# First image of a fused attention kernel: the next input loaded at unit 16, and the split weights made in units without row turns or statistics, those of v partly on GpSimd

## The chip, the cores and the metric

The kernel runs on one core of a Trainium2 chip. The metric is the device time of one execution in microseconds (us), the median over repeated runs. Times inside the kernel are read from one profiled execution; they are counted from the start of its span.

The engines that matter here are TensorE (PE in the profile; its weight loads are PEld), VectorE (DVE), ScalarE (ACT), GpSimd (POOL) and SyncE (SP), whose queue issues nearly all DMAs of this part, strictly in order: an issue that waits for a semaphore holds up all issues behind it.

## The reference, cut to what matters

Two layers over 8 images of 384 channels and 32 x 32 pixels. The change lies in layer 0, an attention with 8 heads of 48 over the 1024 pixels, with a bias that depends on the relative position alone:

```
x   = x + L0(_gn(x), ...)            # _gn: group norm over 32 groups

qkv  = tokens @ qkv_w + qkv_b                       # q, k, v
attn = einsum('bhnd,bhmd->bhnm', q * scale, k)
attn = softmax(attn + relative_bias(h, w, ...), axis=-1)
out  = einsum('bhnm,bhmd->bhnd', attn, v)
out  = out @ proj_w + proj_b
```

Layer 1 (a second attention and a feed-forward block with weights reduced to signs) follows and is not touched.

## The kernel before, in words

Layer 0 is `_layer0`. Images are worked on one after the other. The attention of an image is cut into 32 units, numbered 0 to 31: 4 pairs of heads, two halves of the queries, four groups of keys. Unit u has these steps:

- `scores`: 16 matmuls on TensorE (L746) into two PSUM tiles `s`, one for each head of the pair;
- two additions on VectorE (L757), each of 128 x 1024 elements, that put `s` plus a window of the bias table `grow` into two SBUF tiles `e`;
- two exponentials on ScalarE (L761), in place in `e`;
- `weigh`: 16 matmuls (L777) of `e` with v. TensorE does the weighing of unit u-2 behind the scores of unit u (LAG = 2).

PSUM holds four tiles of this size. One collects the output `o`, so three are left for scores, and the second score tile of a unit takes the place of the first one of the unit before. TensorE can therefore start the scores of unit u+1 only when the first addition of unit u is done.

Everything else is put between the units by an order written out by hand. `later.after(n, work)` issues `work` at the n-th following `later.step()`, and there is one step at the end of every unit. The instructions of such work then stand on each engine's queue behind those of the unit. In the first image (b = 0) this work is:

- **Row pieces and row turns.** The bias table is built while it is in use. `grow_load` (L486) fetches a piece of the table from DRAM with 4 DMAs of 117 KB, in the first image's units into a part of `oT`, and `grow_turn` (L496 on ScalarE, L498 on VectorE, one piece in two each) copies it, with its columns turned round, into `grow`. The last 16 pieces are loaded at the end of v's projection and of the units 0 to 14, and turned two or three units later, on VectorE behind the units 0, 3, 5, 7, 9, 10, 12, 14 and 16.
- **Parts of the weights.** Later images multiply in a faster number format with weights and inputs split into a high part (L108, a mask), a low part (L134, a subtraction), a mix of both (L112), and the low part scaled (L142). For q and k `_cut_weights` does this in four stages for each third k of the rows (128 x 768), with a store of 393 KB to DRAM behind three of them (L122). For v `cut_weights_v` does it on 128 x 384, with stores of 197 KB. All of it is on VectorE.
- **The next input.** `load` (L343) fetches image 1 (three DMAs of 512 KB) into `xn`. `group_norm` then measures it (`bn_stats`, L513, on VectorE, two instructions for each of three stages), sends the statistics through DRAM (L517, L521), aggregates them (L527), computes on GpSimd, sends the result out and back (L535, L539), and applies it on ScalarE (L551).
- **Divisions.** At the end of each pair of heads `divide` sends the row sums through DRAM (L803, L805), inverts them on GpSimd (L806), spreads them by DMA (L810, L818) and multiplies on GpSimd (L822).

The tiles `e`, the mixed parts `cd` and the tiles `cv` of v's parts come from one pool of nine buffers (`etile`). An addition into a new `e` waits until the last user of its buffer is done, a DMA out of it included.

Each DMA on SyncE's queue signals one of eight semaphores in turn, and a DMA waits for the landing of the one eight places before it.

After the units of the first image, TensorE multiplies image 1 with the split weights: `cuts.load` (L161) is issued at unit 28, `wvh` (L986) after the last unit, into the buffer of `wv` itself, and `load_weights_v` (L687) behind that.

Of the kernel before, what the change touches and what calls it, by code (L numbers as in the profile page):

```python
# [22 lines left out]
ALU = mybir.AluOpType  # L23
# [6 lines left out]
B, C, IH, IW = 8, 384, 32, 32  # L30
N = IH * IW
KC = C // P
MT = N // P
HALF = 512
# [29 lines left out]
CUT = 4096.0  # L64
# [41 lines left out]
def _masked(nc, out, of):  # L106

    nc.vector.tensor_single_scalar(out.bitcast(INT), of.bitcast(INT), MASK, op=ALU.bitwise_and)  # L108


def _mixed(nc, out, low, high):
    nc.vector.scalar_tensor_tensor(out, low, -CUT, high, ALU.mult, ALU.add)  # L112


def _cut_weights(nc, k, w, tile, there):

    parts = {}

    def store(i):
        nc.sync.dma_start(  # L122
            there[:, :, i, k].rearrange("n p c -> p n c"),
            parts[i].rearrange("p (n c) -> p n c", c=P),
        )

    def high():
        parts[0] = tile("ch")
        _masked(nc, parts[0], w)
        store(0)  # L130

    def low():
        parts[1] = tile("cl")
        nc.vector.tensor_sub(parts[1], w, parts[0])  # L134

    def mixed():
        parts[2] = tile("cd")
        _mixed(nc, parts[2], parts[1], parts[0])
        store(2)

    def scaled():
        nc.vector.tensor_scalar_mul(parts[1], parts[1], CUT)  # L142
        store(1)

    return [high, low, mixed, scaled]
# [129 lines left out]
def _layer0(tc, ins, x1, sums, shared, weights, beside):  # L275
# [4 lines left out]
    nc = tc.nc  # L280
# [4 lines left out]
    with ExitStack() as ctx:  # L285
# [8 lines left out]
        def etile(name, shape=(P, N), dtype=F32):  # L294
            return ep.tile(list(shape), dtype, tag="e", name=name)
# [4 lines left out]
        later = _Later()  # L300
# [25 lines left out]
        for g in range(P // QT):  # L326
            at = g * QN
# [12 lines left out]
        def load(b):  # L340
            t = shared.image(f"xn{b}")
            for k in range(KC):
                nc.sync.dma_start(t[:, k], x[b, ts(k, P)].rearrange("p h w -> p (h w)"))  # L343
            return t

        first = load(0)
# [13 lines left out]
        wv = const.tile([P, KC, C], F32, tag="wv", name="wv")  # L360
# [236 lines left out]
        cut_v = dram.tile([P, 3, KC, C], F32, tag="cutv", name="cutv", bufs=1)  # L597

        def cut_tile(name):
            return etile(name)[:, 0 : 2 * C]  # L600

        def cut_weights_v(k):

            w = wv[:, k]
            t = etile(f"cv{k}")
            high, mixed = t[:, 0:C], t[:, HALF : HALF + C]

            def first():
                _masked(nc, high, w)
                nc.sync.dma_start(cut_v[:, 0, k], high)  # L610
                nc.vector.tensor_sub(w, w, high)

            def second():
                _mixed(nc, mixed, w, high)
                nc.sync.dma_start(cut_v[:, 2, k], mixed)
                nc.vector.tensor_scalar_mul(w, w, CUT)
                nc.sync.dma_start(cut_v[:, 1, k], w)

            first()
            later.after(2, second)  # L620

        class Ahead:

# [234 lines left out]
        def project_out(b, res, pairs):  # L858
            for m in range(KC):
                products(b, m, pairs)  # L860
                nc.vector.scalar_tensor_tensor(
                    res[m], flat2(pps[b, m]), bp[:, m : m + 1], res[m], ALU.add, ALU.add
                )
                nc.sync.dma_start(x1[b][ts(m, P), :], res[m])
# [4 lines left out]
        stages = group_norm(0, first)  # L869
# [37 lines left out]
        for i in range(len(parts) // 2):  # L907
            later.after(i + (13 if i < 9 else 12), lambda: grow_turns(1))
            at = 1 + i % NF0 if i < 12 else 2 + i % 2
# [4 lines left out]
        for k in range(KC):  # L914
            stages = _cut_weights(
                nc, k, plain[:, ts(k, 2 * C)],
                lambda name, k=k: (
                    spare if name == "ch" else plain[:, ts(k, 2 * C)] if name == "cl"
                    else cut_tile(f"{name}0{k}")
                ),  # L920
                cut,
            )
            for at, stage in zip(((9, 11, 13, 15), (20, 21, 22, 23), (24, 25, 26, 27))[k], stages):
                later.after(at + 1, stage)
        for k in range(KC):
            later.after(17 + k, lambda k=k: cut_weights_v(k))
        for b in range(B):
            held = []
            for i, u in enumerate(units):
                done = held.pop(0) if len(held) == LAG else None  # L930
                held.append(
                    (u, scores(b, qk, u, lambda: weigh(b, *done) if done else None))
                )
                if i == (12 if b == 0 else 1) and b + 1 < B:
                    xn = load(b + 1)
                    for at, stage in zip(
                        (5, 6, 7, 10, 13, *((14, 15) if b == 0 else (13, 13))),
                        group_norm(b + 1, xn),
                    ):
                        later.after(at, stage)  # L940
                if i == 3 and b > 0:
                    project_out(b - 1, residuals(b - 1, etile), range(NF0))
                if b == B - 1:
                    for at, work in beside:
                        if at == i:
                            work()
                later.step()
                if i == 28 and b == 0:
                    cuts = _Cut(
                        nc, cut, BLOCKS,  # L950
                        shared.pool.tile([P, KC * 3 * C], F32R, tag="w", name="wc"),
                    )
                    for n in range(BB):
                        cuts.load(n)
                if b in (1, 2, 3) and i == 12:
                    t = cut_tile(f"cw{b}")
                    weights.load_part(b - 1, t)
                    for at, stage in enumerate(
                        weights.cut(
                            b - 1, t, lambda name, b=b, t=t: t if name == "cl" else cut_tile(f"{name}1{b}")  # L960
                        )
                    ):
                        later.after(4 + at, stage)
                masks, rounds = ((28, 29, 31), ()) if b == 0 else ((25, 26, 27), (28, 29, 30))
                if b + 1 < B:
                    if i == masks[0]:
                        ahead = Ahead(b + 1, xn)
                    if i in masks:
                        ahead.mask(masks.index(i))
                    if i in rounds:  # L970
                        ahead.round(rounds.index(i))

            def weigh_held():
                finish = weigh(b, *held.pop(0))
                if finish is not None:
                    finish()

            if b + 1 == B:
                while held:
                    weigh_held()  # L980
                break
            order = [n % len(BLOCKS) for n in range(b % 2 * BB, b % 2 * BB + len(BLOCKS))]

            if b == 0:
                wh = const.tile([P, KC, C], F32R, tag="wv", name="wvh")
                nc.sync.dma_start(wh.bitcast(F32), cut_v[:, 0])  # L986
                for k in range(KC):
                    ahead.round(k)
            for k in range(2):
                ahead.low(k)  # L990
            weigh_held()
            ahead.low(2)
            ahead.load_weights_v(wh)
            weigh_held()
            for k in range(KC):
                ahead.mixed(k)

            def load_behind(n):
                if n in order[:BB]:
                    cuts.load((n + BB) % len(BLOCKS))  # L1000

            for n in order[:2]:
                for i in range(2):
                    ahead.products(cuts, n, i)
            for n in order[:2]:
                ahead.products(cuts, n, 2)
                ahead.take(n)
                load_behind(n)
            for at, n in enumerate(order[2:], 2):
                for i in (2, 0, 1):  # L1010
                    ahead.products(cuts, n, i)
                ahead.take(n)
                load_behind(n)
                if at == BB - 1:
                    for m2 in range(MT // 2):
                        ahead.project_v(m2)
            qk = ahead.qk
# [8 lines left out]
    def finish():  # L1026
        project_out(B - 1, rest, range(NF0, NP0))
        keep.close()
# [1341 lines left out]
```

## Time and profile before

| What | Value |
|---|---|
| Median of 3 runs | 2956.97 us (2955.67 to 2958.47) |
| The profiled execution: its own time, its span | 2955.07 us, 2953.0 us |
| TensorE busy | 2920.5 us, 99% of the span |
| VectorE busy | 1970.4 us, 67% |
| ScalarE busy | 1505.0 us, 51% |
| GpSimd busy | 491.5 us, 17% |
| Units of the first image: first and last score matmul's stretch | from 76 us to about 200 us |

Busy shares are averages over the whole kernel. The change touches only the 32 units of the first image, some 125 us of 2953, so views with a window on this stretch are the ones to read. In them one pair of L757 additions on VectorE marks one unit, and the distance from pair to pair is the time of a unit. A duration in the profile can reach some hundredths of a microsecond into the next instruction's, so times are best taken from start to start.

### The profile page before, as it was taken

To read this page: it belongs to the slowest core of one execution; us is meant where nothing else is said; L and a number is where in the kernel's file an instruction comes from. 1 tells how busy PE (TensorE), PEld (TensorE's weight loads), DVE (VectorE), ACT (ScalarE), POOL (GpSimd) and SP (SyncE) were. 2 spreads that over 40 slices of the span, in tenths; PEclk is the share of its full clock that TensorE was granted. 3 is DMA by queue.
4 is the path that set the end of the run, shared out by engine and by line. 5 is a ranking of instruction groups with operands and counts; after the bars stand their busy time and mean duration, and the time that the engine had idled before them with its cause. 6 is when DMAs were issued, how large, how long until landed. Compare 5 with 4: busy or idle time off the path is not lost.

```text
span 2953.0 us, 47525 instructions
## 1 busy us (share of the span) xinstructions
PE 2920.5 (99%) x19538; PEld 1694.0 (57%) x19538; DVE 1970.4 (67%) x2005; ACT 1505.0 (51%) x1846; POOL 491.5 (17%) x312
## 2 busy tenths in 40 slices
PE   8999999999999999999999999999999999999998
PEld 3345565657565666644545647647647647655553
DVE  3786858676676757664665775775875875875756
ACT  2553626354453626353553554555555555564644
POOL 2020202111110202112202202302302302301020
PEclk9999999999999999999999999999999999999999
DMA  7643141322213040323311212112112112112111
GB/s 197 175 132 99 45 128 39 114 59 69 76 47 98 24 128 17 93 82 97 87 56 31 83 32 72 67 31 72 67 32 71 67 32 72 67 40 83 40 46 39
DMA packets 131972, 214.36 MB, mean 73 GB/s; under 512 B 62145, under 2 KB 81073, under 8 KB 130369
## 3 DMA queue, kind: packets, MB, share of 16 engines
q1 hardware_dynamic: 128480, 209.39, 24.1%
q8 instruction: 157, 2.57, 0.4%
q10 hardware_dynamic: 3264, 1.82, 0.2%
q14 instruction: 71, 0.57, 0.1%
HBM read 161.83 MB, written 40.28 MB: 68 GB/s over the span
## 4 chain that ended last, share of the span: by engine, by line
PE 91%; DVE 3%; DMA 2%; ACT 2%; issue 1%; SPq 0%; POOL 0%; DVEq 0%; ACTq 0%
PE s L746 15%; PE o L777 15%; PE s L1722 11%; PE o L1771 11%; PE pg L170 6%; PE y2p L2016 6%; PE y1p L1965 5%; PE pp L845 4%; PE pv L1659 4%; PE pm L170 3%; PE pp L1868 3%; PE vg L698 2%; PE pq L1511 2%; PE pq L572 1%; PE vm L698 1%; DVE qk L1592 1%
## 5 line engine op out<-in xcount | busy, mean ns | idle before, releaser
L761 ACT ACTIVATE e<-e 128x1024 f32<-128x1024 f32 x512 | 534.6, 1057 | 347.9 <-DVE e L757 331.2
L757 DVE TENSOR_TENSOR e<-s,grow 128x1024 f32<-128x1024 f32 x512 | 601.3, 1218 | 162.4 <-PE s L746 144.8
L746 PE MATMUL s<-qk 48*64 48x512 f32 x4096 | 613.8, 592 | 7.2 <-DVE e L757 7.2
L777 PE MATMUL o<-e,v 64*64 64x512 f32 x4096 | 608.5, 590 | 1.6 <-DVE e L757 1.6
L1733 ACT ACTIVATE e<-s,kc 128x512 f32<-128x512 f32 x768 | 463.4, 693 | 172.9 <-PE s L1722 161.9
L1722 PE MATMUL s<-qk,qk 64*64 64x512 f32 x3072 | 418.8, 592 | 1.4 <-DVE oT L1781 1.2
L1771 PE MATMUL o<-e,v 64*64 64x512 f32 x3072 | 414.3, 590 | 0.0
L746 PEld LDWEIGHTS s<-qk 48*64 48x64 f32 x4096 | 229.5, 132 | 248.1 <-issue 102.2
L777 PEld LDWEIGHTS o<-e,v 64*64 64x64 f32 x4096 | 250.2, 133 | 196.4 <-issue 105.2
L1722 PEld LDWEIGHTS s<-qk,qk 64*64 64x64 f32 x3072 | 154.2, 132 | 191.0 <-issue 108.5
L1748 DVE TENSOR_TENSOR t<-t,e 128x1024 f32<-128x1024 f32 x192 | 230.9, 1221 | 45.7 <-ACT e L1733 45.5
L1771 PEld LDWEIGHTS o<-e,v 64*64 64x64 f32 x3072 | 160.0, 133 | 168.7 <-issue 141.6
L806 POOL TENSOR_TENSOR inv<-sums,over 128x16 f32<-128x16 f32 x32 | 96.2, 3008 | 850.3 <-DMA sums<-sd 783.3
L1952 DVE TENSOR_REDUCE parts<-y 128x1 f32<-128x1024 f32 x75 | 89.7, 1217 | 102.6 <-ACT y L1949 102.1
L1745 DVE TENSOR_TENSOR t<-e,e 128x1024 f32<-128x1024 f32 x96 | 114.1, 1224 | 57.7 <-ACT e L1733 57.7
L1628 POOL TENSOR_TENSOR hc<-hc,rsqrt 128x32 f32<-128x32 f32 x24 | 138.3, 5761 | 2.0
L1659 PE MATMUL pv<-wv,bx 128*128 128x384 f32 x384 | 128.3, 491 | 0.0
L1868 PE MATMUL pp<-oT,L_attn_proj_wT 128*128 128x512 f32 x288 | 126.3, 595 | 1.7 <-DVE oT L1834 1.7
L845 PE MATMUL pp<-oT,wp 128*128 128x512 f32 x288 | 125.7, 595 | 0.0
L1659 PEld LDWEIGHTS pv<-wv,bx 128*128 128x128 f32 x384 | 119.4, 314 | 9.8 <-ACT e L1733 4.1
L673 DVE SCALAR_TENSOR_TENSOR qk<-pg,qk 128x1024 f32<-128x1024 f32 x42 | 51.5, 1225 | 100.0 <-PE pg L170 73.9
L1965 PE MATMUL y1p<-lun,w 128*128 128x512 f32 x360 | 113.5, 396 | 2.4 <-DVE lun L1915 2.4
(225 smaller groups left out, 3581.5 us busy)
## 6 DMA issues: line engine op xcount, KB each, us to landing
rb<-rd SPq DMA_DIRECT2D x110, 256.0 KB
wc<-there SPq DMA_DIRECT2D x25, 576.0 KB
wc<-cut SPq DMA_DIRECT2D x24, 576.0 KB
xn<-in_x_dram SPq DMA_DIRECT2D x24, 512.0 KB
res<-in_x_dram SPq DMA_DIRECT2D x24, 512.0 KB
x<-res SPq DMA_DIRECT2D x24, 512.0 KB
bx<-x SPq DMA_DIRECT2D x8, 1536.0 KB
rq<-hi SPq DMA_DIRECT2D x48, 256.0 KB
```

The lines of the kernel that those rows point to most:

```text
L170: self.nc.tensor.matmul(out[:, h], w[:, i, k], part[k][:, ts(h, HALF)], start=(k == 0 and i != 1), stop=(k == KC - 1 and i != 0),)
L746: nc.tensor.matmul(s[j][ts(c, QP), i], qk[pair][rows, 1, ts(4 * m2 + 2 * i + c, QP)], qk[pair][rows, 0, ts(h, HALF)], start=True, stop=True,)
L757: nc.vector.tensor_add(e.rearrange("p (i q) -> p i q", i=2), s[j], bass.AP(near.tensor, near.offset, [near.ap[0], [-QROWS * IW, 2], [1, HA ...
L761: nc.scalar.activation(e, e, AF.Exp)
L777: nc.tensor.matmul(po[ts(j, S0), r], v[keys, 2 * m2 + i, 2 * pair + j, :], es[j][keys, ts(i, HALF)], start=(m2 == 0 and i == 0), stop=(m2 ...
L845: nc.tensor.matmul(pps[b, m][:, h], (wp[:, k] if k < NF0 else wl)[:, ts(m, P)], oT[:, k, ts(h, HALF)], start=(k == 0), stop=(k == (NF0 if ...
L1659: nc.tensor.matmul(pv[:, i, 0:C], xt[:, k].rearrange("c (p m) -> c m p", m=MT)[:, 2 * m2 + i], wv[:, k], start=(k == 0), stop=(k == KC - 1),)
L1722: nc.tensor.matmul(s[j][ts(c, QP), i], qk[pair, 1][rows, ts(4 * m2 + 2 * i + c, QP)], qk[pair, 0][rows, ts(h, HALF)], start=True, stop=True,)
L1733: nc.scalar.activation(e[:, ts(i, HALF)], s[j][:, i], AF.Exp, scale=kc[:, pair, j, m : m + 1])
L1748: nc.vector.tensor_add(total[j], total[j], e)
L1771: nc.tensor.matmul(po[ts(j, D1), r], v[keys, 2 * m2 + i, at : at + D1], es[j][keys, ts(i, HALF)], start=(m2 == 0 and i == 0), stop=(m2 == ...
L1965: nc.tensor.matmul(py[m][:, h], w1[:, k, ts(m, P)], un[k][i][:, ts(h, HALF)], start=(k == 0 and i == 0), stop=(k == KC - 1 and i == 1),)
```

## The change

Four things move, all of them in the first image, and some instructions change their engine:

- The load of image 1 is issued at unit 16 and not at unit 12. Its first two measurements come behind the units 17 and 18 (before: 16 and 17), the third with the gathering behind 19 (before: 18), and the aggregation stays behind 21. So does the application, behind 24, 25 and 26.
- The q and k parts: k = 0 at the units 10, 11, 15, 16 (before: 9, 11, 13, 15), k = 1 at 2, 4, 6, 8 (before: 20 to 23), k = 2 at 23, 24, 26, 27 (before: 24 to 27).
- The v parts, which were made in two steps behind the units 16 to 20, are now made in three steps: behind the units 17, 22, 23 for k = 0, behind 21, 25, 26 for k = 1, and behind 27, 30, 31 for k = 2. All stores move to the second and third step.
- Of the v parts, the subtraction and the scaling are on GpSimd; the mask and the mix stay on VectorE.

```diff
         def cut_weights_v(k):
-            w = wv[:, k]
-            t = etile(f"cv{k}")
-            high, mixed = t[:, 0:C], t[:, HALF : HALF + C]
+            w, tiles = wv[:, k], []
 
             def first():
+                tiles.append(etile(f"cv{k}"))
+                high = tiles[0][:, 0:C]
                 _masked(nc, high, w)
+                nc.gpsimd.tensor_sub(w, w, high)
+
+            def second():
+                high, mixed = tiles[0][:, 0:C], tiles[0][:, HALF : HALF + C]
                 nc.sync.dma_start(cut_v[:, 0, k], high)
-                nc.vector.tensor_sub(w, w, high)
-
-            def second():
                 _mixed(nc, mixed, w, high)
+                nc.gpsimd.tensor_scalar(w, w, CUT, 1.0, ALU.mult, ALU.mult)
                 nc.sync.dma_start(cut_v[:, 2, k], mixed)
-                nc.vector.tensor_scalar_mul(w, w, CUT)
+
+            def third():
                 nc.sync.dma_start(cut_v[:, 1, k], w)
 
-            first()
-            later.after(2, second)
+            return first, second, third
...
-            for at, stage in zip(((9, 11, 13, 15), (20, 21, 22, 23), (24, 25, 26, 27))[k], stages):
+            for at, stage in zip(((10, 11, 15, 16), (2, 4, 6, 8), (23, 24, 26, 27))[k], stages):
                 later.after(at + 1, stage)
-        for k in range(KC):
-            later.after(17 + k, lambda k=k: cut_weights_v(k))
+        for k, at in enumerate(((17, 22, 23), (21, 25, 26), (27, 30, 31))):
+            for when, stage in zip(at, cut_weights_v(k)):
+                later.after(when + 1, stage)
...
-                if i == (12 if b == 0 else 1) and b + 1 < B:
+                if i == (16 if b == 0 else 1) and b + 1 < B:
                     xn = load(b + 1)
                     for at, stage in zip(
-                        (5, 6, 7, 10, 13, *((14, 15) if b == 0 else (13, 13))),
+                        (2, 3, 4, 6, 9, 10, 11) if b == 0 else (5, 6, 7, 10, 13, 13, 13),
                         group_norm(b + 1, xn),
                     ):
                         later.after(at, stage)
```

## The prediction

> **What bounds the kernel now.** The page first: TensorE is busy all but 32 us of the span, so a gain must come out of waits of TensorE, or out of slow matmuls.
>
> ```profile
> span 2953.0 us, 47525 instructions
> PE 2920.5 (99%) x19538; PEld 1694.0 (57%) x19538; DVE 1970.4 (67%) x2005; ACT 1505.0 (51%) x1846; POOL 491.5 (17%) x312
> ```
>
> Then TensorE's own waits (who waited for what: us in total, times, longest):
>
> ```profile
> PE ph L445 <- DMA w<-in_L_conv_mlp_w_dram: 8.1, 2, 7.8
> PE s L746 <- DVE e L757: 7.2, 4, 4.4
> ...
> PE o L777 <- DVE e L757: 1.6, 1, 1.6
> ```
>
> All eight images run L746, but a query of the window 80 to 300 us holds the whole 7.2 + 1.6 us. The stall is the first image's alone. Next, the busy times of three stretches of that image's units, and of one piece of the middle one. The columns after the length are PE, PEld, DVE, ACT, POOL, then the granted clock, DMA share and GB/s:
>
> ```profile
> 90.60:124.90 34.30, 34.30 (x321) 15.25 (x317) 29.41 (x31) 24.30 (x28) 2.93 (x1) 1.00 0.59 155
> 121.03:170.08 49.05, 40.30 (x324) 13.47 (x320) 38.82 (x50) 23.18 (x26) 7.99 (x7) 0.93 0.49 145
> 170.08:197.79 27.71, 27.71 (x260) 11.48 (x256) 24.38 (x26) 20.86 (x22) 8.33 (x3) 1.00 0.52 160
> 134.20:140.05 5.85, 5.85 (x28) 1.78 (x32) 3.67 (x4) 3.40 (x4) 0.00 (x0) 0.52 0.54 150
> ```
>
> 170.08 and 197.79 are the starts of the addition pairs of units 23 and 31: 27.71 / 8 = 3.46 us for a unit that TensorE bounds. Units 5 to 13 (93.23 to 121.03) give 3.475. I take 3.47. Units 13 to 23 are the middle stretch: 49.05 us where 10 x 3.47 = 34.7 were due. **14.35 us are lost there**, and nearly nothing elsewhere in the image. VectorE's order of time tells where:
>
> ```profile
> 124.91 2.35 DVE L757 TENSOR_TENSOR e<-s,grow 128x1024 f32<-128x1024 f32 x2
> 132.36 0.65 DVE L498 COPY grow<-oT 128x480 f32<-128x480 f32 x1 [5.11 <-DMA oT<-table]
> 132.93 2.35 DVE L757 TENSOR_TENSOR e<-s,grow 128x1024 f32<-128x1024 f32 x2
> ...
> 163.57 1.23 DVE L757 TENSOR_TENSOR e<-s,grow 128x1024 f32<-128x1024 f32 x1 [2.18 <-PE s L746]
> ```
>
> Pairs start at 121.03, 124.91, 132.93, 137.93, 142.81, 147.73, 152.90, 156.58, 160.18, 166.89, 170.08 (units 13 to 23). Distance less 3.47:
>
> - Units 13, 14: 0.41 + 4.55. The row turn of unit 14 waits 5.11 us for its table piece. SyncE's issues tell why: image 1's input (1.57 MB) goes out at 122.24 to 123.55, that piece at 123.65 to 125.96, behind it.
> - Unit 15: 1.53. After the stall the clock is 0.52 from 134.20 to 140.05.
> - Units 16 to 20: 1.41 + 1.45 + 1.70 + 0.21 + 0.13 = 4.90, VectorE itself. A pair takes 2.27 from start to start, so 3.47 - 2.27 = **1.20 us a unit are free for other work**. Unit 16 has a turn 0.56, v's mask 0.38 and subtraction 0.48, two `bn_stats` 1.19: 2.61, 1.41 too much, which is just the loss. Unit 17 has 2.66, unit 18 2.92.
> - Units 21, 22: 3.24 - 0.28 = 2.96. The second addition of unit 21 starts late, at 163.57. The profile names TensorE, but those scores were long there; the last stores of v's parts out of `cv` buffers are just then under way (L615 took 2.03 us to issue at 160.30). I read it as the wait for a buffer of the nine.
>
> **What the Trainium skill says.** "TensorE: Matmul & The Clock Gate", What's actually happening: after an idle window of about 3.4 us the clock halves until about as long a busy one. The trace agrees: 4.35 us of wait (L746's longest), then 0.52. "GPSIMD Engine Reference", 1. Specifications: GpSimd shares its SBUF interfaces with VectorE. Here a multiply L822 takes 2.38 us beside an idle VectorE and 3.67 beside a busy one, with additions unchanged at 1.2: GpSimd pays. "DMA: Bandwidth & Descriptors", Anatomy of one DMA: some 2.0 us fixed beside the bytes. That section fits another queue's path; here the store of the statistics is issued at 152.15 and the load that waits for it at 154.42, 2.27 us.
>
> **The change, part by part.** Costs are effective ones, start to start.
>
> *VectorE.* Removed: three subtractions (0.48) and three scalings (0.28), 2.3 us. The rest moves. Extras by unit after the change, against 1.20:
>
> - 2: 0.46; 4: 0.87; 6: 0.87; 8: 0.46 (k = 1; no turns there): free.
> - 9: 0.61 + 0.56 = 1.17 (was 1.64); 10: 1.02; 11: 0.87; 13: 0.61 (was 1.48); 14: 0.56; 15: 0.87; 16: 1.02.
> - 17: output sum 0.61 + mask 0.30 + `bn_stats` 1.19 = 2.10, 0.90 too much. 18 and 19: 1.19 each, just in balance.
> - 21: 0.61 + 0.30 + 0.71 = 1.62, 0.42 too much. 22 to 31: at most 1.21.
>
> Single excesses are partly made good: in the trace of before unit 9 had 1.64, 0.44 too much, lost 0.52 and regained 0.21 in the next. So unit 17 costs about 0.6 and 21 about 0.2: **0.8 us left of 4.90**. Units 9 and 25 (1.47, now 1.09) give back 0.15 each, 0.3.
>
> *The table piece of unit 14.* Ahead of it stand only the spread of the first division (L818, 119.98 to 121.80), so it can be issued 1.4 us earlier, and without 1.57 MB in front at 278 GB/s (the rate from 123.0 to 134.2) it lands 5.65 us earlier, by 126.6. The turn comes at 127.2, and 1.20 - 0.56 us of lateness cost nothing: **4.96 and the clock's 1.53 go**. The piece of unit 16 is due later and follows the same way.
>
> *The input at unit 16* stands on SyncE behind the store of k = 0's mix of unit 15. Store and first third, 0.92 MB / 278 = 3.3 us and 2 fixed: 5.3 us after that mix. The first `bn_stats` comes 2.27 + 1.02 + 2.27 + 0.91 = 6.5 us after it. Slack 1.2; later thirds need 1.9 each and get 3.46. Cost zero; if wrong, 1 to 3 us, all of it in VectorE's full units.
>
> *Statistics' way.* Gathering to aggregation is now two units, 6.9 us; before, 152.15 to about 156.5 sufficed (4.4).
>
> *Buffers.* `cv` of k = 0 lives from 17 to its stores behind 22. These stand on SyncE behind L535 and L539, which wait for GpSimd (aggregation + 2.95 us before). They land about 6.1 us after the aggregation; unit 24's second addition, the first that wants the buffer, comes 7.7 after it. k = 1's and the mix `cd` of 26 have 2 to 3 us to spare at 28. **2.96 goes**, with 0 to 2 us left if that slack is too small.
>
> *GpSimd* gets three subtractions (2634 ns for 1152 columns, so 0.88 for 384) and three scalings (1196 for 1024, 0.45), 4.0 us, among 16 us of its own work. Nobody waits within a unit. Bound: 0 to 4.0 us if VectorE were locked out for all of it; I take 0. *SyncE* keeps its number of DMAs. k = 1's stores join table pieces whose turns come three units later. ScalarE keeps its work.
>
> *The sum:* 0.41 + 4.55 + 1.53 + 4.90 + 2.96 = 14.35 lost; 0.8 remains, 0.3 comes back elsewhere: 13.8 us. The profiled execution would take 2955.07 - 13.8 = 2941.3. It is 1.9 below the median of before, 2956.97, which gives **2943.2**.
>
> **The rivals.**
>
> *One transfer is still late* (row piece at 14, `bn_stats` at 17, or a buffer at 24): the slacks are 0.6, 1.2 and 1.6 us, smaller than the guesses they rest on are sure. Price 2 to 6 us: 2945 to 2949.
>
> *The stall only moves*: the pieces themselves are the limit (DMA share 0.96 in 123.0:134.2), a turn waits 5 us at 14 or 16 and the clock falls as before. Against it: turns of 9, 10 and 12 waited for nothing. Only the overload and the buffer wait (4.9 - 0.8 + 2.96 = 7.1) would go, less another late transfer: about 2951 to 2956.
>
> *Slower.* v's last third is stored only behind unit 31, after GpSimd's scaling, and `wvh`, the load into `wv`'s own buffer, then `wx`, sums and the fourth `wc` block stand behind that store on SyncE. Before, `wvh` was issued at 192.55, 5.2 us ahead of unit 31's pair. Now it goes out about 4.7 after it, and `wx` (before at 204.17, 6.4 after) lands near 14.7: 6.4 + 1.18 and 0.59 MB at 278 GB/s (6.3) + 2. v's products began at 216.33, 18.5 after. Slack 3.8. It decides from a GpSimd or SyncE delay of 3.8 us on, and the kernel is slower when that exceeds 17.6; with 20 us it takes 2959. GpSimd's queue there holds 8 us of work in 17, so it is unlikely.
>
> **How the numbers follow.** All slacks hold: 0.70, 2941 to 2945. One late transfer: 0.18. The stall only moves: 0.08, a quarter of it still faster by 0.2% (5.9 us, about what a measurement of this kernel can tell from no change). Slower: 0.04. So faster 0.70 + 0.18 + 0.02 = 0.90, same 0.06, slower 0.04; range 2939.5 (nothing at all lost, 15 us, and run scatter) to 2950 (the first two cases with a unit's stall).
>
> **What would show it.** Right: L498 without a DMA wait; TensorE's wait for L757 below 2 us; clock 1.00 from 121 on; pairs 13 to 23 in about 35.5 us; first pg matmul at 189 to 190 and not 203. Wrong: an L513 or L757 that waits for a DMA, a vm L698 that waits for `wx` or `wvh`, additions above 1.2 us beside GpSimd's new work.

## The result, and the profile after

| | median | range | runs |
|---|---|---|---|
| before | 2955.93 us | 2954.09 to 2958.47 | 6 |
| after | 2942.23 us | 2940.6 to 2943.48 | 6 |

The ratio is 0.9953, with a 95% interval of 0.994 to 0.9966: the medians differ by 13.7 us, and the interval reaches from about 10 to 18 us. The profiled execution took 2940.60 us, its span is 2939.1 us.

The page's first lines, after. The part of the span in which TensorE is not busy fell from 32.5 to 25.5 us, and its busy time by 6.9.

```profile
span 2939.1 us, 47521 instructions
PE 2913.6 (99%) x19538; PEld 1703.0 (58%) x19538; DVE 1969.8 (67%) x1999; ACT 1504.5 (51%) x1846; POOL 493.5 (17%) x318
```

TensorE's own waits (who waited for what: us in total, times, longest). The additions, L757 before, are L759 now. The scores waited 7.2 us for them and the weighing 1.6; what is left is 1.8 us for the scores and no line for the weighing.

```profile
PE ph L445 <- DMA w<-in_L_conv_mlp_w_dram: 7.9, 2, 7.5
PE y1p L1968 <- DVE lun L1918: 3.0, 7, 0.5
PE s L748 <- DVE e L759: 1.8, 2, 1.4
```

Busy times by stretch. The columns after the length are PE, PEld, DVE, ACT, POOL, granted clock, DMA share, GB/s. The second stretch is the units 13 to 23 (119.20 and 156.70 are the starts of their addition pairs), the third the units 23 to 31. Before, the second took 49.05 us at a clock of 0.93; now it takes 37.50 at 1.00. The third was 27.71 and is 27.30.

```profile
90.60:119.20 28.60, 28.60 (x272) 13.95 (x268) 26.23 (x30) 21.09 (x24) 2.92 (x1) 1.00 0.64 178
119.20:156.70 37.50, 36.96 (x337) 16.51 (x329) 35.08 (x38) 23.30 (x26) 11.10 (x9) 1.00 0.50 135
156.70:184.00 27.30, 26.04 (x243) 14.11 (x247) 25.06 (x29) 20.53 (x21) 8.06 (x6) 1.00 0.50 158
```

VectorE's order of time, after (start, duration, what it did; in brackets the idle time just before it):

```profile
122.63 2.36 DVE L759 TENSOR_TENSOR e<-s,grow 128x1024 f32<-128x1024 f32 x2 [0.33 <-PE s L748]
125.88 0.65 DVE L498 COPY grow<-oT 128x480 f32<-128x480 f32 x1 [0.90 <-DMA oT<-table]
126.45 2.34 DVE L759 TENSOR_TENSOR e<-s,grow 128x1024 f32<-128x1024 f32 x2
...
135.50 0.69 DVE L790 TENSOR_TENSOR oT<-o,oT 128x512 f32<-128x512 f32 x1
136.11 0.35 DVE L108 TENSOR_SCALAR cv<-wv 128x384 int32<-128x384 int32 x1
136.37 1.28 DVE L513 BATCH_NORM_STATS2 gst<-xn 128x6 f32<-128x512 f32 x2
...
151.65 2.28 DVE L759 TENSOR_TENSOR e<-s,grow 128x1024 f32<-128x1024 f32 x2
153.86 2.91 DVE L112 SCALAR_TENSOR_TENSOR cv<-wv,cv 128x384 f32<-128x384 f32 x1
156.70 2.34 DVE L759 TENSOR_TENSOR e<-s,grow 128x1024 f32<-128x1024 f32 x2
```

The turn of unit 14 waits 0.90 us for its table piece and not 5.11, and the next pair follows 3.82 us after the one before: the stall is gone. The measurement of image 1 (L513) starts without a wait at 136.37. **The mix L112 at 153.86 is new: it takes 2.91 us**, where the same instruction took 0.54 or 0.55 in the kernel before (VectorE's order of time, before):

```profile
155.16 0.55 DVE L112 SCALAR_TENSOR_TENSOR cv<-wv,cv 128x384 f32<-128x384 f32 x1
```

What each unit loses: the distance from its pair to the next, less 3.47 us, for the units 13 to 22. The starts are taken unrounded from the trace, so an entry can differ by 0.01 from the lines shown:

| unit | 13 | 14 | 15 | 16 | 17 | 18 | 19 | 20 | 21 | 22 | units 13 to 23 |
|---|---|---|---|---|---|---|---|---|---|---|---|
| before | 0.41 | 4.55 | 1.53 | 1.42 | 1.44 | 1.70 | 0.21 | 0.13 | 3.24 | -0.28 | 49.05 |
| after | -0.03 | 0.35 | -0.22 | 0.04 | 0.89 | -0.02 | -0.02 | -0.16 | 0.41 | 1.57 | 37.50 |

The stretch gives 11.55 us, the units 0 to 13 0.37 (43.09 before, 42.72 after) and 23 to 31 0.41: 12.33 in all. Unit 22 lost nothing before and now loses more than any other.

### The profile page after: what moved, and what is told of

Same layout as the page of the kernel before. It is cut to its first block, busy times and chain, and to the rows that moved or that the text cites. A ratio compares the mean times of both kernels' runs of the same rounds, so it can differ in the third digit from the quotient of the medians.

```text
span 2939.1 us, 47521 instructions
## 1 busy us (share of the span) xinstructions
PE 2913.6 (99%) x19538; PEld 1703.0 (58%) x19538; DVE 1969.8 (67%) x1999; ACT 1504.5 (51%) x1846; POOL 493.5 (17%) x318
## 4 chain that ended last, share of the span: by engine, by line
PE 92%; DVE 3%; DMA 2%; ACT 2%; issue 1%; SPq 0%; POOL 0%; DVEq 0%; ACTq 0%
PE s L748 15%; PE o L779 15%; PE s L1725 11%; PE o L1774 10%; PE pg L170 6%; PE y2p L2019 6%; PE y1p L1968 5%; PE pp L847 4%; PE pv L1662 4%; PE pm L170 3%; PE pp L1871 3%; PE vg L700 2%; PE pq L1514 2%; PE pq L572 1%; DMA rb<-rd 1%
## 5 line engine op out<-in xcount | busy, mean ns | idle before, releaser
L759 DVE TENSOR_TENSOR e<-s,grow 128x1024 f32<-128x1024 f32 x512 | 601.1, 1218 | 154.6 <-PE s L748 137.8
L748 PE MATMUL s<-qk 48*64 48x512 f32 x4096 | 606.4, 590 | 1.8 <-DVE e L759 1.8
```

The lines of the kernel that those rows point to most:

```text
L748: nc.tensor.matmul(s[j][ts(c, QP), i], qk[pair][rows, 1, ts(4 * m2 + 2 * i + c, QP)], qk[pair][rows, 0, ts(h, HALF)], start=True, stop=True,)
L759: nc.vector.tensor_add(e.rearrange("p (i q) -> p i q", i=2), s[j], bass.AP(near.tensor, near.offset, [near.ap[0], [-QROWS * IW, 2], [1, HA ...
```

## The experiments

Each kernel was compared with runs of the kernel before on the same chip. Two sets ran: the first four below beside a before of 2954.89 us, the last four beside one of 2955.88.

### The late load alone

In the kernel before:

```diff
-                if i == (12 if b == 0 else 1) and b + 1 < B:
+                if i == (16 if b == 0 else 1) and b + 1 < B:
...
-                        (5, 6, 7, 10, 13, *((14, 15) if b == 0 else (13, 13))),
+                        (2, 3, 4, 6, 9, 10, 11) if b == 0 else (5, 6, 7, 10, 13, 13, 13),
```

> The kernel before with one part of the change: image 1 loaded at unit 16, measured behind 17, 18, 19; the weights' parts as before, all on VectorE. Theory (the losses add up by cause): the wait of unit 14's row turn (4.96 us) and the low clock after it (1.53) go, the overload of VectorE stays (extras of units 16 to 21: 1.42, 2.66, 2.91, 2.05, 1.32, 2.19 against 1.20 each, 5.3 us over), a buffer wait of 0 to 3 us stays: 6 to 9 us faster than before. Rival (VectorE's overload hides behind the stall): 12 us or more.

Measured: 2946.36 us (2944.75 to 2947.97), ratio 0.9973 (0.9962 to 0.9983), 8.5 us faster. In VectorE's order of time of this kernel the turn that waited 5.11 us waits 0.23:

```profile
126.77 0.65 DVE L498 COPY grow<-oT 128x480 f32<-128x480 f32 x1 [0.23 <-DMA oT<-table]
```

By unit, from 13: 0.41, -0.22, -0.03, 0.22, 1.45, 1.69, 1.03, 0.13, 0.97, -0.28. The stall (4.55) and the slow clock after it (1.53) are gone: the granted clock is 1.00 in all of these units. The excesses of VectorE stay, that of unit 13 (0.41) where it was, most of the others moved by one unit. Unit 21 falls from 3.24 to 0.97 though nothing of v's parts was moved, so the late load alone is enough to remove its wait.

### The moved parts alone

The same two edits taken back in the kernel after, so that the load is again at 12.

> The other part alone: the weights' parts as after the change, image 1 loaded at unit 12 and measured behind 16, 17, 18 as before. Theory: unit 14's turn still waits some 5 us for its piece and the clock still falls to about 0.5 behind it (6.5 us lost), of the overload about 1.6 us are left, of a GpSimd lock 0 to 1.6; 4 to 6.5 us faster than before. Rival (the early stores of k = 1 and the input now meet, the wait grows): 2 us or less.

Measured: 2949.95 us (2948.3 to 2952.12), ratio 0.9984 (0.9977 to 0.9991), 4.9 us faster. VectorE's order of time:

```profile
132.45 0.65 DVE L498 COPY grow<-oT 128x480 f32<-128x480 f32 x1 [6.57 <-DMA oT<-table]
...
163.10 2.89 DVE L112 SCALAR_TENSOR_TENSOR cv<-wv,cv 128x384 f32<-128x384 f32 x1
```

The table piece is late again, by 6.57 us: the input ahead of it on SyncE's queue makes this stall, not the work on VectorE. Unit 14 loses 6.02, 1.47 more than before. Counted from the start of unit 0, VectorE comes to that turn 0.8 us earlier, and the piece lands 0.65 later; why it lands later is not shown (in "Buffers for v's parts elsewhere", which changes nothing so early, unit 14 lost 5.07). The mix is slow here too, beside the same multiply of GpSimd that the next experiment tests. The two halves, 8.5 and 4.9, make 13.4, about the whole 13.7, though both take away the wait at unit 21 (3.24 - 0.97 = 2.27). The stall that grew by 1.47 in this kernel hides most of that double count.

### GpSimd's old multiply made short

What else ran at 153.86? GpSimd's order of time in the kernel after:

```profile
153.56 0.46 POOL L533 COPY gof<-gmv 32x24 f32<-32x24 f32 x1
153.99 2.36 POOL L824 TENSOR_TENSOR oT<-oT,rb 128x1024 f32<-128x1024 f32 x1
156.85 0.51 POOL L616 TENSOR_SCALAR wv<-wv 128x384 f32<-128x384 f32 x1 [0.50 <-DVE cv L112]
```

The multiply of the second division (L822 before, L824 now) runs from 153.99 to 156.35 at its undisturbed length, and the mix ends just after it. VectorE seems to stand still for the whole of it. The test shortens that one multiply in the kernel after; the division of the pair's other columns is left out:

```diff
+            n = 32 if b == 0 and pair == 1 else N
...
-            nc.gpsimd.tensor_mul(o, o, rb[0])
+            nc.gpsimd.tensor_mul(o[:, 0:n], o[:, 0:n], rb[0][:, 0:n])
```

> After the change, with GpSimd's multiply of the second pair of heads of the first image (L822 before, behind unit 21) cut to 32 of 1024 columns; the division of the rest of that pair is left out. Theory (the mix L112 of unit 22, which took 2.91 us and not 0.55, was locked out of SBUF by that multiply, which ran 153.99 to 156.35): L112 falls to 0.55 us, units 22 to 23 take 3.5 us and not 5.05, 1.5 us less than after the change. Rival (L112 waited for the subtraction L610 on GpSimd, or for its own write): L112 stays at about 2.9 and the time at that of after the change.

Measured: 2940.15 us (2939.36 to 2940.35), ratio 0.9951 (0.9937 to 0.9964). That is 14.7 us below its before; the kernel after was 13.7 and 14.3 below in its two comparisons, so the time alone does not show the effect. The trace does:

```profile
154.65 0.62 DVE L112 SCALAR_TENSOR_TENSOR cv<-wv,cv 128x384 f32<-128x384 f32 x1
```

The mix takes 0.62, unit 22 loses -0.29 and not 1.57, and the units 13 to 23 take 35.45 us. The old multiply is the cause of the slow mix.

### Buffers for v's parts elsewhere

The prediction read unit 21 of the kernel before as a wait for a pool buffer. Here, in the kernel before, two of v's three parts get tiles outside that pool:

```diff
-            t = etile(f"cv{k}")
-            high, mixed = t[:, 0:C], t[:, HALF : HALF + C]
+            t = plain[:, 0 : 2 * C] if k == 1 else spare if k == 0 else etile(f"cv{k}")
+            high, mixed = t[:, 0:C], t[:, C : 2 * C]
```

> The kernel before with one edit: v's parts of k = 0 and k = 1 do not lie in the pool of nine buffers but in parts of the first weights' tile that are free by then. Theory (the late second addition of unit 21, 163.57, waited for the stores out of a cv buffer): that addition follows the first without a gap, and 2.5 to 3 us go. Rival (it waited for the scores on TensorE, as the profile names it): no gain, the gap of 2.18 us stays.

Measured: 2952.75 us (2950.54 to 2954.34), ratio 0.9993 (0.9984 to 1.0001). The medians differ by 2.1 us, but the interval holds 1, so the time leaves it open. In VectorE's order of time the pair of unit 21 is whole, where before its second addition came 2.18 us late:

```profile
158.73 2.35 DVE L757 TENSOR_TENSOR e<-s,grow 128x1024 f32<-128x1024 f32 x2
161.00 0.68 DVE L788 TENSOR_TENSOR oT<-o,oT 128x512 f32<-128x512 f32 x1
```

Unit 21 loses 0.97 and not 3.24. The wait was for a pool buffer, and 2.27 us of it. The 0.97 is plain excess: in the kernel before, an output sum (0.60), a subtraction (0.87) and the aggregation (0.71) stand behind that pair, 2.18 us where 1.20 are free.

### The kernel after, once more

No edit; it is the measure for the three kernels below.

> The changed kernel itself once more, to stand on the same chip beside the next three. Every theory: 12 to 14 us faster than before, units 13 to 23 in 37.5 us with 5.0 for unit 22 (the lock-out of L112 repeats if it comes from the order of the queues; if it was an accident of one execution, unit 22 takes 3.5).

Measured: 2941.62 us (2941.24 to 2942.06), ratio 0.9951 (0.9938 to 0.9965), 14.3 us faster and so a little over the 12 to 14 expected. Unit 22 loses 1.57 here too, with a mix of 2.90 us: the slow mix was no accident of one execution.

### v's subtraction and scaling back on VectorE

In the kernel after:

```diff
-                nc.gpsimd.tensor_sub(w, w, high)
+                nc.vector.tensor_sub(w, w, high)
...
-                nc.gpsimd.tensor_scalar(w, w, CUT, 1.0, ALU.mult, ALU.mult)
+                nc.vector.tensor_scalar_mul(w, w, CUT)
```

> After the change, with the subtractions and scalings of v's parts back on VectorE and everything else as after. Theory (free time of 1.20 us a unit): extras grow by 0.56 in unit 17 (to 2.66) and 21 (to 2.18), by 0.28 in 22, 25, 30 and 0.56 in 27; 1 to 2 us slower than after the change, so 10.5 to 12.5 faster than before. Rival (GpSimd's help is what makes the change work): 4 us or more slower than after.

Measured: 2942.65 us (2941.86 to 2945.42), ratio 0.9957 (0.9943 to 0.9971), by medians 1.0 us slower than the kernel after, with ranges that overlap by 0.2. The units 13 to 23 take 38.73 us where the repeated kernel after took 37.36. So GpSimd's help is worth about 1 us, and the mix is slow without GpSimd's new work (GpSimd's order of time, then VectorE's):

```profile
154.79 2.68 POOL L824 TENSOR_TENSOR oT<-oT,rb 128x1024 f32<-128x1024 f32 x1
```

```profile
155.34 2.54 DVE L112 SCALAR_TENSOR_TENSOR cv<-wv,cv 128x384 f32<-128x384 f32 x1
```

### The mix one unit later

In the kernel after, the second stage of v's first third moves from 22 to 23, and the third stage with it:

```diff
-        for k, at in enumerate(((17, 22, 23), (21, 25, 26), (27, 30, 31))):
+        for k, at in enumerate(((17, 23, 24), (21, 25, 26), (27, 30, 31))):
```

> After the change, with the second and third step of v's k = 0 behind units 23 and 24 and not 22 and 23. Theory (the mix is locked out by the multiply that starts at the end of unit 22's pair): the mix takes 0.55 us behind unit 23, where 0.46 + 0.47 us lie well below 1.20, and unit 22 takes 3.2 to 3.5 us: 1.5 to 2 us faster than after the change. Rival (GpSimd's next instruction or the later buffer takes the wait over, at unit 23 or at the second addition of 25): no gain, a wait of 1 us or more there.

Measured: **2939.78 us** (2939.39 to 2940.84), ratio 0.9946 (0.9932 to 0.9959). It is 1.84 us below the kernel after in the same set, with ranges that do not overlap, and faster than both kernels of this case. GpSimd's order of time, then VectorE's:

```profile
155.43 2.38 POOL L824 TENSOR_TENSOR oT<-oT,rb 128x1024 f32<-128x1024 f32 x1
```

```profile
158.77 0.55 DVE L108 TENSOR_SCALAR w<-w 128x768 int32<-128x768 int32 x1
159.24 0.55 DVE L112 SCALAR_TENSOR_TENSOR cv<-wv,cv 128x384 f32<-128x384 f32 x1
```

The multiply ends at 157.81, the mix starts at 159.24 and takes 0.55. Unit 22 loses -0.28, and the units 13 to 23 take 35.65 us.

### The first steps of v's parts spread further

In the kernel after, with the mix at 23 as above and two masks moved away from the full units 17 and 21:

```diff
-        for k, at in enumerate(((17, 22, 23), (21, 25, 26), (27, 30, 31))):
+        for k, at in enumerate(((20, 23, 24), (22, 25, 26), (27, 30, 31))):
```

> As e4_mix_at_23, and the masks of v's k = 0 and k = 1 move from the full units 17 and 21 to 20 and 22, which have nothing else. Extras of 17 and 21 fall to 1.80 and 1.32 us. Theory: 0.4 to 0.8 us faster than e4_mix_at_23, units 13 to 23 in about 35 us. Rival (GpSimd's subtraction, now at 20 and 22, stands in front of the statistics or the multiply and makes them late): no gain over e4.

Measured: 2940.79 us (2939.89 to 2942.1), ratio 0.9948 (0.9935 to 0.9962). That is no gain on the kernel above but 1.0 us more, with ranges that overlap: the expectation was wrong. The two full units did gain, 0.27 us each (17 lost 0.62, 21 lost 0.14). GpSimd's and VectorE's order of time:

```profile
154.49 2.37 POOL L824 TENSOR_TENSOR oT<-oT,rb 128x1024 f32<-128x1024 f32 x1
```

```profile
155.03 2.05 DVE L108 TENSOR_SCALAR cv<-wv 128x384 int32<-128x384 int32 x1
```

One mask now stands behind unit 22, in the mix's old place, and takes 2.05 us where it took 0.35. Unit 22 loses 0.70 and not -0.28, which is more than the two units gained, and unit 14 lost 0.55 where it lost 0.35 above. I had taken a mask, which reads only one tile, to be safe there.

## Why the prediction was right, and where it was off

The forecast was 2943.2 us, 13.8 below the kernel before; the median came out at 2942.23, 13.7 below, within the likeliest case. Its steps:

- **The table piece and the clock** (4.96 + 1.53): right. Units 13 to 15 lose 0.41 + 4.55 + 1.53 = 6.49 before and 0.10 after. The late load alone takes this away but for the 0.41, and without it the stall returns. The 0.41 of unit 13 was wrongly counted to the piece: it is an excess of VectorE, an output sum (0.61) and a mix (0.87) behind one pair, and stays when only the load moves. The turn waits 0.90 us where none was forecast, so one of the prediction's signs of being right did not come. Counted from the start of unit 0 the piece lands 5.0 us earlier, not 5.65, and VectorE is at the turn 0.8 us sooner than before, which the prediction had not counted. Unit 14 loses 0.35 and unit 15 gives 0.22 of that back.
- **The excesses of VectorE** (4.90, of which 0.8 was to remain): right in kind. Unit 17 cost 0.89 and not 0.6, unit 21 0.41 and not 0.2: just their excess over 1.20, with no discount in the unit itself. Unit 18 gave nothing back, though I had counted on that; unit 22, which could have, was filled by the slow mix (with the mix at 23 it gave back 0.28).
- **The buffer** (2.96): right that it goes, wrong in what it was. 2.27 was the wait and 0.97 excess of unit 21, of which unit 22 gave back 0.28. Each half of the change takes the wait away by itself.
- **GpSimd at 0: the mis-sized term.** The prediction had "with additions unchanged at 1.2: GpSimd pays", read from one multiply of before, and asked only whether GpSimd's new instructions would hold up VectorE. They did not: none of VectorE's instructions beside them took longer. But the change also moved a mix to where GpSimd's old multiply falls, and there VectorE paid: 153.86 to 156.70 is 2.84 us of VectorE where 1.20 are free, 1.64 too much, and unit 22 lost 1.57. The shortened multiply and the mix one unit later show that this pair of instructions is the cause, and the run with the subtractions back on VectorE that GpSimd's new work is not.
- **The sum for the stretch.** 0.8 us was to be lost in the units 13 to 23; it is 37.50 - 34.70 = 2.80, and 1.57 of it is unit 22. So the stretch gave 11.55 of a forecast 13.55.
- **Elsewhere** 0.78 came where 0.3 was forecast: the units 9 and 25 lost 0.52 and 0.36 before and lose nothing now.
- **The end value agreed better than its terms, and that is in part luck.** The units give 12.33 us, and 2955.07 - 2940.60 is 14.47 between the profiled executions. Of that, 1.46 is the start of unit 0, at 77.94 before and 76.48 after. The same kernel after began unit 0 at 78.37 in its second profile, so this is scatter between executions and no effect of the change. The last 0.7 lies after the units (0.1) and outside the span (0.6). The 13.7 of the medians exceeds the 12.33 as well, but their interval holds it; no run places the difference.
- **The rivals.** No transfer made L513 or L759 wait. The stall did not move to the units 9 to 16. The slower case did not come: `wvh` was issued at 188.76 and `wx` at 190.38, 4.76 and 6.38 us after unit 31's pair; the first matmul with the split weights (`pg`) came 5.4 us after that pair, as before, and v's products, at 202.27, waited for neither load.

## What to carry to other kernels

Work that is moved between units meets new neighbours on other engines: before an instruction is put into a free place, look at what GpSimd does at that moment, old work included, and not only at what the change adds. Here a stall on a DMA that stood behind a large load on an in-order queue was cured by the order of the issues, and moving the compute beside it did not shorten it. Where one engine's slack per unit is known (3.47 - 2.27 us here), an excess in a single unit is best counted whole; in these runs at most 0.3 us of it came back in the next unit.

## What the runs showed of the hardware that I had not expected

**VectorE can stand still for a whole GpSimd instruction.** The mix (two SBUF inputs) went from 0.55 to 2.91 us, the mask (one SBUF input) from 0.35 to 2.05, each beside a multiply of 2.36 or 2.37 us that kept its own undisturbed length. For the mix the shortened multiply shows that this is the reason; for the mask only the coincidence does. The Trainium skill, "SBUF — State Buffer", Who interferes with whom, says that VectorE and GpSimd share a pair of ports, taken for a whole instruction, while the other one blocks fully; on VectorE's side it names instructions with two SBUF inputs, and forms such as `tensor_scalar` in fast modes that use both ports. The mix agrees. The mask fits if it runs in such a mode. Its pace speaks for that (from 136.11 to 136.37 for 384 columns, 0.7 ns a column, beside 1.1 ns for the additions, 2.27 us for a pair), and so does a multiply of the kernel before that was recorded at 194.13, 0.25 us after a mask, and took 2.67 us and not 2.38; but no run tests it. The additions and L513, each with at most one SBUF input, kept their times beside GpSimd, again as that section has it.

**Which of the two loses cannot be read from the recorded starts.** In the kernel before, the multiply is recorded first and loses (GpSimd's, then VectorE's order of time):

```profile
168.61 3.67 POOL L822 TENSOR_TENSOR oT<-oT,rb 128x1024 f32<-128x1024 f32 x1
```

```profile
169.09 0.94 DVE L112 SCALAR_TENSOR_TENSOR cd<-w 128x768 f32<-128x768 f32 x1
```

In the kernel after, the mix is recorded first, at 153.86 against 153.99, and loses. The same section says that the first to issue wins. The records neither confirm nor refute it, since they do not show when a port is taken. Nor does the distance tell: in the run with the subtractions back on VectorE the multiply is recorded 0.55 us ahead of the mix, nearly the 0.48 of the kernel before, and it is the mix that loses most (2.54 us, the multiply 2.68). From the one case of before I had concluded that GpSimd always pays; this was one outcome of two.
